# Another start for the first unit's triangular inverse, extra matmuls ahead of idle stretches, and new planner constants

## The chip, the core and the metric

The kernel runs on one core of one Trainium2 chip. The metric is the device time of one execution in microseconds. Over three runs the median was 804.33 us (802.57 to 809.08). One further execution was profiled: it took 806.73 us, and 804.9 us lie between its first and its last instruction (its span). All rows below come from that execution, so sums are made against its 804.9 us.

## What is computed

One transformer-like block over 32 sequences of 256 tokens and 128 features, in four steps, each with a layer norm ahead of it and a residual around it:

```
x = x + attn_a(layernorm(x))      # delta-rule recurrence, below
x = x + ffn(layernorm(x))         # silu(x Wg) * (x Wu), times Wd; hidden 384
x = x + attn_b(layernorm(x))      # Mamba-2 style: conv of 4, silu, chunked state space, gated norm
x = x + ffn(layernorm(x))
```

The change sits in the first step. Its recurrence over the tokens of a sequence is

```
S   = S @ (a_t * (I - b_t * k_t k_t^T)) + b_t * v_t k_t^T
o_t = (q_t @ S) * g_t
```

with a, b and g sigmoids of linear maps of x, and k of unit length. The kernel doesn't walk over tokens. It takes 128 tokens at a time as one chunk, where the recurrence becomes a triangular system: with N the strictly triangular 128x128 matrix of -k_i.k_j times a decay, the inverse X of (I - N) is what the rest of the step multiplies by. Two sequences, so four chunks, are one unit of work, and there are 16 units.

## The kernel before

**Planner.** Every operation of all 16 units goes into a list with its engine, an estimated cost and its predecessors (`Planner.add`, L203; the helpers `matmul`, `transpose`, `act`, `vec`, `pool`, `dma` call it, so the lines that the profile shows are theirs: L238 matmul, L251 transpose, L259 and L261 ScalarE, L275 VectorE, L292 GpSimd, L302 DMA issue). `Planner.run` (L333) then places the operations one by one on PE, DVE, ACT, POOL and the SP queue: of those that could start first, the one with the smallest due time. The due time comes from a unit's place (`at`, L328: period times unit, plus SHIFT of that unit), the longest path to the unit's end, and STAGE for the four steps. HOP is the time that it assumes for a dependence between engines, SLACK the time until a buffer is free again, SWITCH the penalty for a ScalarE table load, KEEP the penalty for a change between matmuls of wide and of narrow weights, EARLY how long before its operands are ready an operation may claim a PSUM bank. Each engine executes its instructions in the planned order, so a wait holds back all that is queued behind it. At the end the order is sorted by planned start and emitted (L441).

**Inverse of a unit** (`attention`, L737). The matrices N of the four chunks stand side by side as `neg_a`. The 16x16 diagonal blocks are inverted by substitution: 8 DMAs on SP write the blocks to DRAM (`blocks_a`, L854), 8 more bring them back, one copy for each of 16 partitions (`rows_a`, L861); then VectorE does 15 pairs of small operations, one pair for each row of a block (`step_a`, `u_a`, L871); GpSimd spreads the result with the mask `blk` into the 128x128 inverse (`x_a`, L881). Then a loop over LEVELS = (16, 32) doubles the block size (L891):

```
for lv, d in enumerate(LEVELS):
    ...                                   # 4 transposes of x_a -> pt_a (PE)
    copy(t_halves[..., 1, :], pt...)      # ACT
    ...                                   # 4 matmuls neg_a, t_a -> p_a (PE)
    copy(t_halves[..., 0, :], p1)         # ACT
    ...                                   # 4 matmuls t_a, x_a -> p_a (PE)
    vec("copy_predicated", halves[..., 1, :], mask_x[lv], p3, ...)   # DVE, into x_a
```

A last level of 64 is written out separately (with `pair`), and then `wq_a`, `z_a`, `po_a`, `py_a` lead to the step's output x1, whose feed-forward step begins with the matmuls `fg_f`.

With SHIFT[0] = 18900 and SHIFT[1] = -4200 against a period of 17900, unit 1 is due before unit 0, and goes first through all of this. The plan is built twice, once for a second path (matmuls with unrounded weights) that these inputs don't take.

Of the kernel before, what the change touches and what calls it, by code (L numbers as in the profile page):

```python
# [11 lines left out]
I32 = mybir.dt.int32  # L12
# [10 lines left out]
BLOCK = 16  # L23
NBLK = P // BLOCK
LEVELS = (16, 32)
HALF = P // 2


# [119 lines left out]
class Planner:  # L148
# [2 lines left out]


    SLOTS = {"ps": 8, "m": 56, "l": 10, "t": 12, "s": 64, "d": 6, "g": 6, "b": 3, "e": 4}
    SWITCH = 76800.0
    HOP, SLACK = 30.0, 130.0
    STAGE = (0.0, -8900.0, 1900.0, 0.0)
    EARLY = 0.0
    SPARE = {"ps": 0.5, "m": 3, "l": 0.5, "t": 1, "s": 2, "d": 0.5, "g": 0.5, "b": 0.5, "e": 0.5}
    LAST = 0.12
    SHIFT = (18900.0, -4200.0, 0.0, 0.0, 1500.0, 11400.0, 1600.0, 1500.0, 0.0, 0.0, 19300.0, -27800.0, -1400.0, -9200.0, -7200.0, -5400.0)  # L160
    HALF = "be"
    RATE = 270.0
    LANES = 8
    CUT = 150.0
    KEEP = 3900.0
    SIZES = {"ps": 512, "m": 512, "l": 1024, "t": 64, "s": 32, "d": 512, "g": 8192, "b": 384, "e": 12288}

    def __init__(self, tc, pools, period, window):
# [34 lines left out]
    def add(self, eng, busy, late, emit, outs, ins, table=None, after=(), lock=False):  # L203
        op = Op()
        op.eng, op.busy, op.late, op.emit, op.table, op.lock = eng, busy, late, emit, table, lock
        op.unit, op.n, op.stage = self.unit, len(self.ops), self.stage
        op.preds, op.succs, op.bufs = {p.n: p for p in after}, [], []
        op.moves, op.cut, op.batch = 0.0, 0, ()
# [61 lines left out]
    def copy(self, out, in_):  # L270
        self.act(out, in_, AF.Copy)
# [12 lines left out]
    def pool(self, name, out, *args, ins=(), cost=None, **kw):  # L284
        n = _count(out)
        if cost is None:
            cost = {
                "tensor_tensor": 1.66 * n + 149, "tensor_scalar": n + 260, "tensor_copy": n + 190, "memset": 0.97 * n + 60,
            }.get(name, n / 2 + 100)

        def emit():
            getattr(self.tc.nc.gpsimd, name)(real(out), *map(real, args), **{k: real(v) for k, v in kw.items()})  # L292
# [19 lines left out]
    def gates(self):  # L312
# [7 lines left out]
        for b, ops in users.items():  # L320
# [4 lines left out]
                    of.add(self.ops[n])  # L325
            b.gate = {p for op in ops for p in op.preds.values()} - of

    def at(self, unit):  # L328

        late = max(0, unit - (self.units - 3))  # L330
        return (unit - late + late * self.LAST) * self.period + self.SHIFT[unit]

    def run(self):  # L333
# [105 lines left out]
                oldest += 1  # L439
        self.span = max(op.done for op in ops)  # L440
        order.sort(key=lambda op: (op.start, op.n))  # L441
        with self.tc.manual_schedule():
            for op in order:
                for b in op.bufs:
                    if b.tile is None:
                        size = self.SIZES[b.kind]
                        flat = self.pools[b.kind].tile([1 if b.kind in "dge" else P, size], BF16 if b.kind in self.HALF else F32, tag=f"{b.kind}{b.slot[1]}", name=b.name + self.mark)
                        b.tile = flat[:, : b.size]
# [13 lines left out]
def hybrid_block(ctx: ExitStack, tc: tile.TileContext, ins: dict, out: bass.AP):  # L462
# [43 lines left out]
            pattern=pattern, channel_multiplier=by,  # L506
        )

    ident = pl.const([P, P], "ident")
    pool("memset", ident, 0.0)  # L510
    select(ident, ALU.not_equal, 0, [[-1, P]], 1, fill=1.0)

# [14 lines left out]

    mask_x = []  # L530
    for d in LEVELS:
        nb = P // (2 * d)
        m = pl.const([P, nb, d], f"m_{d}")
        pool("memset", m, 1.0)
        select(m, ALU.is_ge, 0, [[-2 * d, nb], [0, d]], 1)
        select(m, ALU.is_ge, d - 1, [[2 * d, nb], [0, d]], -1)
        mask_x.append(m.bitcast(I32)[:, None, :, :].to_broadcast([P, NT, nb, d]))

# [156 lines left out]
    def bc(t, n):  # L695

        return t[:, None, :].to_broadcast([P, n, t.shape[1]])
# [39 lines left out]
    def attention(g, x):  # L737
# [113 lines left out]

        blocks = pl.buf("g", [1, NBLK * NT * BLOCK * BLOCK], f"blocks_{n}")  # L854
        for b in range(NBLK):
            at = slice(b * BLOCK, (b + 1) * BLOCK)
            pl.dma(
                blocks[0, :].rearrange("(b t j i) -> b j t i", b=NBLK, t=NT, i=BLOCK)[b, :, :, :],
                diag[:, :, at].part(at), late=1400,
            )  # L860
        rows_n = pl.buf("l", [P, NT, BLOCK, BLOCK], f"rows_{n}")  # L861
        spread = rows_n.rearrange("p t j i -> p (t j i)")
        for b in range(NBLK):
            at = slice(b * BLOCK, (b + 1) * BLOCK)
            size = NT * BLOCK * BLOCK
            pl.dma(
                spread.part(at),
                blocks[0, b * size : (b + 1) * size].via(lambda ap: ap.partition_broadcast(BLOCK)),
                late=2100,
            )  # L870
        u = pl.buf("t", [P, NT, BLOCK], f"u_{n}")  # L871
        pool("tensor_copy", u, bc(eye, NT), cost=254)
        for j in range(BLOCK - 1):
            w = BLOCK - 1 - j
            step = pl.buf("t", [P, NT, w], f"step_{n}_{j}")
            vec(
                "tensor_tensor", step, rows_n[:, :, j, j + 1 :],
                u[:, :, j : j + 1].to_broadcast([P, NT, w]), ALU.mult,
            )
            vec("tensor_tensor", u[:, :, j + 1 :], u[:, :, j + 1 :], step, ALU.add)  # L880
        xi = big([P, 2, SEQS, P], f"x_{n}")  # L881
        xi_f = xi.rearrange("p c s t -> p (c s) t")
        pool(
            "tensor_tensor", xi_f.rearrange("p t (b i) -> p t b i", b=NBLK),
            u[:, :, None, :].to_broadcast([P, NT, NBLK, BLOCK]),
            blk[:, None, :, :].to_broadcast([P, NT, NBLK, BLOCK]), ALU.mult, cost=1215,
        )

        for lv, d in enumerate(LEVELS):  # L891
            nb = P // (2 * d)
            halves = xi_f.rearrange("p t (b h e) -> p t b h e", h=2, e=d)
            pt = bank([P, NT, P], f"pt_{n}_{d}")
            for j in range(NT):
                pl.transpose(pt[:, j, :], xi_f[:, j, :], ident)

            t = big([P, NT, P], f"t_{n}_{d}")
            t_halves = t.rearrange("p t (b h e) -> p t b h e", h=2, e=d)
            copy(t_halves[:, :, :, 1, :], pt.rearrange("p t (b h e) -> p t b h e", h=2, e=d)[:, :, :, 0, :])  # L900
            p1 = bank([P, NT, nb, d], f"p1_{n}_{d}")
# [6 lines left out]
            vec("copy_predicated", halves[:, :, :, 1, :], mask_x[lv], p3, ins=(xi_f,), more=17)  # L908

# [333 lines left out]
```

## Time and profile before

| what | us |
|---|---|
| median of three runs (range) | 804.33 (802.57 to 809.08) |
| profiled execution / its span | 806.73 / 804.9 |
| PE busy | 744.7 |
| DVE busy | 684.3 |
| ACT busy | 597.2 |
| of it 66 table loads of 1283 ns | 84.7 |
| POOL busy | 364.0 |
| 240 + 240 `step_a` and `u_a` on DVE, 216 and 227 ns | 106.0 |
| mean granted TensorE clock | 0.975 |

A busy time is the sum over an engine's instructions. A matmul in float32 appears as two records, and the records of a row overlap, so the time that PE needs for work is better read from the distance of starts than from the durations. The profile's stretches of time list, for each engine, busy us with the number of instructions in brackets, then the clock that TensorE was granted (1.00 is full), the DMA share and GB/s. In the timeline a row gives start, duration, engine, line, operation, out<-in, shapes and count, and in square brackets the idle time before it with what ended it.

Where PE was idle (length of a stretch less PE busy in it): 9.9 us in 0 to 40, 12.1 in 40 to 80, 1.4 in 80 to 120, 4.7 in 120 to 160, some 18 in the 560 us from 160 to 720, and 14.3 from 720 to the end.

### The profile page before, as it was taken

The numbers are of one execution on the slowest core, as the hardware profiler recorded it, in microseconds if no ns is written. First come the engines' busy times: TensorE is split into PE (matmuls) and PEld (weight loads), VectorE is DVE, ScalarE is ACT, GpSimd is POOL, SyncE is SP. The second block draws the span as 40 slices with busy tenths as digits, with TensorE's granted clock in tenths as the row PEclk, the third lists the DMA queues.
The fourth block names the chain that finished last, engine by engine and source line by source line (L and its number), as shares of the span: only waits on it lengthen the run. The fifth ranks groups of instructions, "written<-read, shape, count | busy, mean of one in ns | idle before, by whom it ended". The sixth has DMA issues, their size and how long they took to land.

```text
span 804.9 us, 16786 instructions
## 1 busy us (share of the span) xinstructions
PE 744.7 (93%) x5485; PEld 616.5 (77%) x5485; DVE 684.3 (85%) x2386; ACT 597.2 (74%) x1443; POOL 364.0 (45%) x597
## 2 busy tenths in 40 slices
PE   5958999899999999999999999899999999998886
PEld 4646886687878888877988878686789988776775
DVE  4794799989988889889999689989898778999964
ACT  5833467979687877779787798897955578997862
POOL 8994332262452815514732634646631123243550
PEclk9976999999999999999999999999999999999999
DMA  5221110010110002101011002011201000000001
GB/s 145 82 68 42 29 42 1 5 33 1 56 30 24 22 7 67 42 27 33 18 30 31 27 15 58 16 45 44 67 4 43 14 5 1 5 15 5 13 10 44
DMA packets 42159, 25.48 MB, mean 32 GB/s; under 512 B 18448, under 2 KB 37840, under 8 KB 42064
## 3 DMA queue, kind: packets, MB, share of 16 engines
q1 hardware_dynamic: 41056, 24.13, 11.1%
q8 instruction: 45, 0.74, 0.4%
q14 instruction: 50, 0.41, 0.2%
q10 hardware_dynamic: 1008, 0.20, 0.1%
HBM read 19.16 MB, written 5.14 MB: 30 GB/s over the span
## 4 chain that ended last, share of the span: by engine, by line
PE 52%; DVE 20%; ACT 15%; POOL 5%; issue 3%; DMA 2%; SPq 1%; ACTq 0%; DVEq 0%; POOLq 0%
PE p_a L238 6%; PE fy_f L238 5%; DVE cy_s L275 4%; PE fy_h L238 4%; PE fg_f L238 3%; ACT L261 3%; PE sy_ps_s L238 3%; PE so_s L238 2%; PE fu_f L238 2%; PE pc_s L238 2%; PE fg_h L238 2%; PE fu_h L238 2%; PE pt_a L251 2%; DVE u_a L275 2%; PE cb_ps_s L238 2%
## 5 line engine op out<-in xcount | busy, mean ns | idle before, releaser
L275 DVE SCALAR_TENSOR_TENSOR cy_s<-pc_s,cw,cy_s 128x510 f32<-128x510 f32 (+2 forms) x192 | 137.6, 731 | 2.9 <-ACT cy_s L261 2.3
L261 ACT ACT_TABLE_LOAD x66 | 84.7, 1283 | 9.9 <-DMA x<-in_L_attn_a_x_dram 5.8
L238 PE MATMUL fy_f<-wdT,hT_f 128*128 128x128 f32 x384 | 74.5, 280 | 0.0
L238 PE MATMUL fy_h<-wdT,hT_h 128*128 128x128 f32 x384 | 72.1, 281 | 0.6 <-DVE hT_h L275 0.3
L238 PEld LDWEIGHTS fy_f<-wdT,hT_f 128*128 128x128 f32 x384 | 61.4, 191 | 6.3 <-issue 3.6
L238 PE MATMUL pc_s<-xT_s,w_xbc 128*128 128x512 f32 x128 | 64.5, 599 | 1.3 <-ACT gT_s L259 0.7
L238 PEld LDWEIGHTS fy_h<-wdT,hT_h 128*128 128x128 f32 x384 | 59.1, 191 | 8.1 <-issue 4.3
L275 DVE TENSOR_TENSOR step_a<-rows_a,u_a 128x16 f32<-128x16 f32 (+14 forms) x240 | 51.7, 216 | 7.5 <-DMA rows_a<-blocks_a 3.1
L275 DVE TENSOR_TENSOR u_a<-u_a,step_a 128x16 f32<-128x16 f32 (+14 forms) x240 | 54.3, 227 | 3.9
L261 ACT ACTIVATE cy_s<-pc_s,cb,cw 128x512 f32<-128x512 f32 x64 | 48.3, 779 | 9.3 <-PE pc_s L238 9.1
L292 POOL TENSOR_TENSOR xd_s<-xt_s,dt_s 128x512 f32<-128x512 f32 x32 | 33.2, 1045 | 42.9 <-ACT xt_s L259 42.2
L238 PE MATMUL so_s<-w_out,gT_s 128*128 128x128 f32 x256 | 45.8, 290 | 1.9 <-DVE cy_s L275 1.2
L238 PEld LDWEIGHTS so_s<-w_out,gT_s 128*128 128x128 f32 x256 | 39.7, 204 | 6.6 <-ACT cy_s L261 1.4
L261 ACT ACTIVATE sc_s<-cy_s 128x512 f32<-128x512 f32 x64 | 38.9, 636 | 3.6 <-DVE cy_s L275 1.9
L275 DVE SCALAR_TENSOR_TENSOR sm_s<-pl_s,cb_s 128x512 f32<-128x512 f32 x64 | 41.3, 680 | 0.3 <-ACT pl_s L261 0.2
L292 POOL TENSOR_TENSOR sy_s<-sy_s,yo_s 128x256 f32<-128x256 f32 x32 | 24.6, 773 | 35.5 <-DVE sy_s L275 14.2
L238 PEld LDWEIGHTS p_a<-t_a,neg_a 128*128 128x128 f32 x256 | 36.4, 203 | 5.5 <-ACT t_a L259 3.7
L238 PE MATMUL p_a<-t_a,neg_a 128*128 128x64 f32 x256 | 38.1, 280 | 1.8 <-DVE x L275 1.3
L238 PEld LDWEIGHTS p_a<-x_a,t_a 128*128 128x128 f32 x256 | 36.6, 201 | 3.7 <-ACT t_a L259 2.3
L238 PE MATMUL p_a<-x_a,t_a 128*128 128x64 f32 x256 | 37.9, 274 | 1.0 <-ACT t_a L259 1.0
L259 ACT COPY t_a<-pt_a 128x256 f32<-128x256 f32 (+1 forms) x64 | 20.2, 316 | 24.0 <-PE pt_a L251 22.9
L275 DVE TENSOR_TENSOR hT_f<-fth_f,fu_f 128x512 f32<-128x512 f32 x48 | 31.2, 681 | 7.3 <-PE fu_f L238 4.8
(253 smaller groups left out, 2420.7 us busy)
## 6 DMA issues: line engine op xcount, KB each, us to landing
rows_a<-blocks_a SPq DMA_DIRECT2D x128, 64.0 KB
x<-in_L_attn_a_x_dram SPq DMA_DIRECT2D x16, 256.0 KB
dec_a<-row_a SPq DMA_DIRECT2D x16, 256.0 KB
out_dram<-x SPq DMA_DIRECT2D x16, 256.0 KB
blocks_a<-neg_a SPq DMA_DIRECT2D x128, 4.0 KB
cuts_s<-cut_s SPq DMA_DIRECT2D x48, 8.0 KB
sums_t<-cuts_s SPq DMA_DIRECT2D x32, 12.0 KB
sums_s<-cuts_s SPq DMA_DIRECT2D x16, 24.0 KB
```

Source lines behind the costliest of these rows:

```text
L238: self.tc.nc.tensor.matmul(real(out), lhsT=real(lhsT), rhs=real(rhs), start=start, stop=stop)
L251: self.tc.nc.tensor.transpose(real(out), real(in_), real(ident))
L259: self.tc.nc.scalar.copy(real(out), real(in_))
L261: self.tc.nc.scalar.activation(real(out), real(in_), func, bias=real(bias), scale=real(scale), **kw)
L275: getattr(self.tc.nc.vector, name)(real(out), *map(real, args), **{k: real(v) for k, v in kw.items()})
L292: getattr(self.tc.nc.gpsimd, name)(real(out), *map(real, args), **{k: real(v) for k, v in kw.items()})
```

## The change

1. The unit with g = 0 no longer uses substitution. Its inverse starts as the identity (a ScalarE copy), the elements beside the diagonal of the 2x2 blocks are put in by one `copy_predicated`, and the loop over levels runs over 2, 4, 8, 16, 32 in place of 16, 32. So for this unit 16 DMAs on SP, 30 VectorE operations and two GpSimd operations go, and 3 levels (each with 12 PE operations, 2 ScalarE copies and 1 VectorE copy), a ScalarE copy and a VectorE copy come. GpSimd makes four more masks (4 memsets, 8 selects).
2. `keep_busy` walks over PE's planned order. Where the plan has PE idle for over 300 ns ahead of an operation that is the first to write its PSUM bank, it puts int(0.7 gap / 223) matmuls of the identity with itself into that bank just before it. They come to 122 in the path that runs: 20 ahead of PE's first operation, 10 more up to unit 0's first `fg_f`, 92 later (7 of these with 8 columns, the others with 128).
3. Planner constants: SWITCH, HOP, SLACK, STAGE, EARLY, LAST, SHIFT, KEEP. Unit 0 now goes first. The order of instructions changes on every engine; ACT's table loads go from 66 to 74.

```
+EARLY_UNITS = 1
+EARLY_LEVELS = (1, 2, 4, 8)
...
-    SWITCH = 76800.0
-    HOP, SLACK = 30.0, 130.0
-    STAGE = (0.0, -8900.0, 1900.0, 0.0)
-    EARLY = 0.0
+    SWITCH = 118100.0
+    HOP, SLACK = 70.0, 70.0
+    STAGE = (-1800.0, -7600.0, 1900.0, 0.0)
+    EARLY = 700.0
...
-    LAST = 0.12
-    SHIFT = (18900.0, -4200.0, 0.0, 0.0, 1500.0, 11400.0, 1600.0, 1500.0, 0.0, 0.0, 19300.0, -27800.0, -1400.0, -9200.0, -7200.0, -5400.0)
+    LAST = 0.1
+    SHIFT = (17000.0, 3100.0, 0.0, 0.0, 1500.0, 11400.0, 1600.0, 1500.0, -4200.0, 0.0, 6700.0, -27800.0, -1400.0, -9200.0, -7200.0, -6000.0)
...
-    KEEP = 3900.0
+    IDLE, WARM = 300.0, 0.7
+    KEEP = 2000.0
...
+    def keep_busy(self, order):
+        written, free = set(), 1700.0
+        for op in order:
+            if op.eng != "PE":
+                continue
+            bank = next(b for b in op.bufs if b.kind == "ps")
+            gap = op.start - free
+            if gap > self.IDLE and bank not in written and not op.cut:
+                op.warm, op.bank = int(gap * self.WARM / 223), bank
+            written.add(bank)
+            free = op.start + op.busy
...
+                for _ in range(op.warm):
+                    n = min(P, op.bank.size)
+                    one = self.ident.real()
+                    self.tc.nc.tensor.matmul(op.bank.flat[:, :n], lhsT=one, rhs=one[:, :n], start=True, stop=True)
                 op.emit()
...
-    for d in LEVELS:
+    for d in EARLY_LEVELS + LEVELS:
...
+        if g < EARLY_UNITS:
+            copy(xi_f, bc(ident, NT))
+            later = lambda v: v.rearrange("p t (b h e) -> p t b h e", h=2, e=1)[:, :, :, 1, :]
+            vec("copy_predicated", later(xi_f), mask_x[1], later(diag), ins=(xi_f,), more=17)
+        else:
...
-        for lv, d in enumerate(LEVELS):
+        for d in (EARLY_LEVELS[1:] if g < EARLY_UNITS else ()) + LEVELS:
```

The branch after `else` is the substitution as it was.

More of the change, by code (lines that the diff above doesn't have):

```diff
@@ L207, in add @@
         op.preds, op.succs, op.bufs = {p.n: p for p in after}, [], []
-        op.moves, op.cut, op.batch = 0.0, 0, ()
+        op.moves, op.cut, op.batch, op.warm = 0.0, 0, (), 0
         for v, write in [(v, False) for v in ins] + [(v, True) for v in outs]:
@@ L441, in run @@
         order.sort(key=lambda op: (op.start, op.n))
+        self.keep_busy(order)
         with self.tc.manual_schedule():
@@ L447, in run @@
                         flat = self.pools[b.kind].tile([1 if b.kind in "dge" else P, size], BF16 if b.kind in self.HALF else F32, tag=f"{b.kind}{b.slot[1]}", name=b.name + self.mark)
-                        b.tile = flat[:, : b.size]
+                        b.flat = b.tile = flat[:, : b.size]
                         if len(b.dims) > 2:
@@ L507, in select @@
         )
-    ident = pl.const([P, P], "ident")
+    ident = pl.ident = pl.const([P, P], "ident")
     pool("memset", ident, 0.0)
@@ L526, in hybrid_block @@
     vec("tensor_reduce", eye, ident.rearrange("p (b i) -> p i b", i=BLOCK), AX.X, ALU.add, n=P)
-    mask_x = []
-    for d in LEVELS:
+    mask_x = {}
+    for d in EARLY_LEVELS + LEVELS:
         nb = P // (2 * d)
@@ L536, in hybrid_block @@
         select(m, ALU.is_ge, d - 1, [[2 * d, nb], [0, d]], -1)
-        mask_x.append(m.bitcast(I32)[:, None, :, :].to_broadcast([P, NT, nb, d]))
+        mask_x[d] = m.bitcast(I32)[:, None, :, :].to_broadcast([P, NT, nb, d])
     parts = 2 * NH * 3
@@ L849, in attention @@
         diag = neg[:, :2, :, :].rearrange("p c s t -> p (c s) t")
[L854 to L880, printed above, removed]
@@ L881, in attention @@
         xi = big([P, 2, SEQS, P], f"x_{n}")
         xi_f = xi.rearrange("p c s t -> p (c s) t")
[L883 to L887, printed above, removed]
-        for lv, d in enumerate(LEVELS):
+        if g < EARLY_UNITS:
[3 more added lines that the diff above has]
+        else:
+            blocks = pl.buf("g", [1, NBLK * NT * BLOCK * BLOCK], f"blocks_{n}")
+            for b in range(NBLK):
+                at = slice(b * BLOCK, (b + 1) * BLOCK)
+                pl.dma(
+                    blocks[0, :].rearrange("(b t j i) -> b j t i", b=NBLK, t=NT, i=BLOCK)[b, :, :, :],
+                    diag[:, :, at].part(at), late=1400,
+                )
+            rows_n = pl.buf("l", [P, NT, BLOCK, BLOCK], f"rows_{n}")
+            spread = rows_n.rearrange("p t j i -> p (t j i)")
+            for b in range(NBLK):
+                at = slice(b * BLOCK, (b + 1) * BLOCK)
+                size = NT * BLOCK * BLOCK
+                pl.dma(
+                    spread.part(at),
+                    blocks[0, b * size : (b + 1) * size].via(lambda ap: ap.partition_broadcast(BLOCK)),
+                    late=2100,
+                )
+            u = pl.buf("t", [P, NT, BLOCK], f"u_{n}")
+            pool("tensor_copy", u, bc(eye, NT), cost=254)
+            for j in range(BLOCK - 1):
+                w = BLOCK - 1 - j
+                step = pl.buf("t", [P, NT, w], f"step_{n}_{j}")
+                vec(
+                    "tensor_tensor", step, rows_n[:, :, j, j + 1 :],
+                    u[:, :, j : j + 1].to_broadcast([P, NT, w]), ALU.mult,
+                )
+                vec("tensor_tensor", u[:, :, j + 1 :], u[:, :, j + 1 :], step, ALU.add)
+            pool(
+                "tensor_tensor", xi_f.rearrange("p t (b i) -> p t b i", b=NBLK),
+                u[:, :, None, :].to_broadcast([P, NT, NBLK, BLOCK]),
+                blk[:, None, :, :].to_broadcast([P, NT, NBLK, BLOCK]), ALU.mult, cost=1215,
+            )
@@ L907, in attention @@
                 matmul(p3[:, j, :, :], t[:, j, :], halves[:, j, :, 1, :], True, True)
-            vec("copy_predicated", halves[:, :, :, 1, :], mask_x[lv], p3, ins=(xi_f,), more=17)
+            vec("copy_predicated", halves[:, :, :, 1, :], mask_x[d], p3, ins=(xi_f,), more=17)
         up, low = slice(0, HALF), slice(HALF, P)
```

## The prediction

> **What bounds the kernel now.** I read the page first: PE is busy 93% of the span, DVE 85%. Then its slices, because a mean over stages hides where the rest lies.
>
> ```profile
> PE   5958999899999999999999999899999999998886
> DVE  4794799989988889889999689989898778999964
> PEclk9976999999999999999999999999999999999999
> ```
>
> From the fifth slice (80 us) to the last four PE is full: there PE bounds the kernel, and only less PE work, fewer small stalls or a faster clock help. The weak slices are the first four, and the clock is low in the third and fourth. So next the stretches around each drop of the clock:
>
> ```profile
> 44.50:47.90 3.40, 0.59 (x4) 0.42 (x4) 3.19 (x7) 0.00 (x0) 3.25 (x5) 1.00 0.50 146
> 47.90:58.10 10.20, 6.25 (x22) 4.92 (x22) 9.90 (x28) 2.82 (x6) 10.08 (x16) 0.50 0.21 68
> 61.60:65.00 3.40, 1.53 (x7) 0.65 (x6) 3.23 (x15) 1.83 (x11) 1.21 (x6) 0.99 0.04 4
> 65.00:78.60 13.60, 12.30 (x54) 11.27 (x55) 4.12 (x16) 3.65 (x11) 8.53 (x11) 0.50 0.22 61
> ```
>
> The first number behind the length is PE's busy time, the last but two the clock. PE was 17% and 45% busy in the 3.4 us ahead of two drops, then ran 10.2 and 13.6 us at half speed. What PE waited for is in the timeline of the four engines and SP:
>
> ```profile
> 31.42 3.62 SPq L302 DMA_DIRECT2D blocks_a<-neg_a  x8
> 35.08 3.67 SPq L302 DMA_DIRECT2D rows_a<-blocks_a  x8
> ...
> 41.30 0.64 DVE L275 TENSOR_TENSOR step_a<-rows_a,u_a 128x60 f32<-128x60 f32 x1 [0.22 <-DMA blocks_a<-neg_a]
> ...
> 54.93 0.50 DVE L275 TENSOR_TENSOR u_a<-u_a,step_a 128x4 f32<-128x4 f32 x1
> ...
> 57.18 1.25 POOL L292 TENSOR_TENSOR x_a<-u_a,blk 128x512 f32<-128x512 f32 x1
> ...
> 61.11 0.60 PE L251 MATMUL pt_a<-ident,x_a 128*128 128x128 f32 x4
> ...
> 103.61 0.72 PE L238 MATMUL fg_f<-xT_f,wgT 128*128 128x512 f32 x2
> ```
>
> The first unit's `neg_a` (unit 1 is first in the old order, unit 0 in the new) is ready at 31.4 us. Its 16 DMAs, 30 DVE operations and the GpSimd spread take until 58.4, and level 16 starts at 61.1. The first feed-forward matmul starts at 103.6.
>
> **What PE's work costs.** Distances of starts, at full clock: a float32 matmul of 128 columns takes two records and 0.21 us (four `fy_h` at 790.36, 0.84 to the next start), a 64-column one of the levels no less (four in 0.94 at 99.42); I use 0.22 for both, and 0.11 for a transpose (four in 0.44 at 109.75). At half clock the 128-column matmul takes 0.43 (row at 14.57, four matmuls in 1.74 to the next start), so PE is cold until about 17 us, although the clock column has no record there.
>
> ```profile
> 14.57 1.95 PE L238 MATMUL pk_a<-wkab,xT_a 128*128 128x131 f32 x8
> 16.31 1.46 PE L251 MATMUL xT_ps_a<-ident,xn_a 128*128 128x128 f32 x8
> ...
> 99.42 1.10 PE L238 MATMUL p_a<-t_a,neg_a 128*128 128x64 f32 x8
> 100.36 0.44 PE L238 MATMUL kk_a<-kT_a 128*128 128x128 f32 x2
> ```
>
> Counting the instructions of the two orders at such distances (0.86 for 512 float32 columns, 0.43 for 256, 0.23 for an `fg`/`fu` matmul), the program before holds 680 us of PE work, 62 of it ahead of the first `fg_f`. That starts at 103.6, so 41 us are lost by then; the other 618 take 701 us.
>
> **Part 1, the first unit.** Gone: 3.62 + 3.67 us of SP issue with their landing, 30 DVE operations of 216 to 227 ns (6.6 us), two GpSimd operations. Added: 3 levels. A level at full clock is the row of `pt_a` at 82.18 up to the end of `copy_predicated` at 86.81, 4.6 us; at half clock, 61.11 to 69.90, 8.8. I take 4.6, since PE has other units' work between the steps and fillers: `neg_a` at about 32 (its chain is unchanged, but some more bn statistics are queued ahead on DVE), the first element step 1 us, 3 x 4.6 = 14, so level 16 starts at 47 to 48, not 61.1. From there to `fg_f` the trace took 42.5 us, 13.6 of them at half clock with 12.3 busy. At full clock 6.2 of that goes; also 1.5 to 2 of the idle rows between. That gives 47.5 + 34 = 82 for `fg_f`. A check from the work: 64 us stand ahead of it in the new order, with 10 fillers (2 us) after PE's first operation; from 8 us on that makes 74 without any stall, so 82 leaves 8 us for stalls. Gain 21.6; the ends are 9.0 (three levels at 8.8: `fg_f` at 94.6) and 25.6 (half the stalls: 78). SP: the second unit's `blocks_a` no longer queue behind the first unit's 16 DMAs (issued at 38.86, their `neg_a` ready at 35.6), and its DVE pairs come in 36 to 57 us, so its level 16 can follow when the first unit's level 64 ends. SP's wait for the scalar `large` moves: it stood behind both units' blocks, and now stands ahead of `dec_a` of unit 2 and of unit 1's blocks. DVE writes `large` at 40.93 now, from a matmul at 40.61 that the new order has ahead of the first `kk_a`, so before 31; I cost it at nothing, and if it were late, unit 1 would be, while unit 0's levels fill PE. The identity copy (ACT, about 0.6) runs while ACT waits for x, idle until 5.80; the 12 more mask operations (0.15 to 0.26 each, some 2.5 us) move POOL's first `rstd_a`, which waited for DVE statistics at 6.25 and now gets about 1 us late: that is inside the stall allowance. Behind the first `fg_f`, PE has 623 us of work where it had 618: +5.0.
>
> **Part 2, fillers.** 20 ahead of PE's first real matmul (8.05 now) start at about 1.7 us, when `ident` is there; at half clock 0.43 x 20 = 8.7 ends at 10.4, at full clock 6.1. With a clock that rises on the way they end about when the weights land: cost 0 to 2.4 us, taken 0 (ends by 8.5); PE's cold stretch to 17 us goes, about 3 us of PE time, which is within the 82. The 92 later ones: 85 x 0.22 plus 7 small ones, 19 to 20 us. In a real gap they cost nothing; on a busy PE all. PE's own idle after 103.6 is some 37 us, so most have room, but the plan's gaps need not be there. I take a quarter, +5 (ends 0 and 20). They write only to the bank of the operation behind them, so they add no wait, just length.
>
> Against that stands the clock. Later drops:
>
> ```profile
> 727.20:730.60 3.40, 1.39 (x13) 1.08 (x11) 3.40 (x11) 3.40 (x10) 3.21 (x5) 0.99 0.00 0
> 730.60:734.00 3.40, 3.24 (x10) 2.36 (x11) 3.19 (x12) 2.42 (x8) 1.85 (x3) 0.50 0.00 0
> ```
>
> and the same at 242.4, 754.5 and 771.5, PE busy 3.1 to 3.4 in each: 13.2 us of busy PE at half clock, 6.6 lost. I take -5 of them (0 to -6.6). Here a rule speaks against the fills. The Trainium skill, "TensorE: Matmul & The Clock Gate", section "Why this matters for your kernels", has the clock fall when PE idles for over some 3 us between bursts. By it the gap of 4.48 us ahead of 47.31 costs clock, but the fills behind the front buy none, the -5 goes and the sum gives 794. The trace differs: ahead of 65.0 the longest idle row is 0.92 us, ahead of 242.4 it is 1.07, and yet the clock fell, after 3.4 us with PE 45% and 63% busy. So I follow the rows: share of work, not one long gap.
>
> **Part 3, new order.** 8 more table loads of 1283 ns are 10.3 us of ACT, which has 26% idle and carries 15% of the chain that ended last: +1.5 (0 to 10). The rest of the order (HOP, SLACK, due times) I can't cost from the trace: the stages follow each other after the same amount of PE work in both orders to within 10 us, so 0, with -8 to +8 for it: of the 701 us after `fg_f`, 83 are not work by my distances, and a tenth of that either way is my guess.
>
> **Sum.** -21.6 + 5.0 + 5 - 5 + 1.5 = -15.1 against 804.9 of span. The profiled run is 2.4 us above the median, so from 804.33: 789.
>
> **Rivals.** (a) The front's gain is given back: 16 units pass DVE, 80 to 90% busy and more from 80 us on, and what starts 20 us earlier waits there. For it: DVE at 95% in 360 to 440. Against: it loses 6.6 us of work, and PE, not DVE, is full in those slices, idle for 1 to 4 us in each 80. If two thirds of the 21.6 are lost: 804.3 - 15.1 + 14.4 = 804. (b) Slower: the fillers and the doubling fall on a busy PE. 92 fillers at full price 20, doubling 5.0, table loads on the chain 10.3: 35 against 21.6 from the front and 5 of clock: 804.3 - 26.6 + 35.3 = 813. It decides from where more than two thirds of the planned gaps are not real while ACT's loads hold PE up. For it: the plan's 223 ns for a matmul is what PE takes, but it allows for no micro-stalls, so PE may be late at most places. Against: other engines are late then too. (c) The change doesn't do what it says: fillers late, the clock falls as before, levels at 8.8: `fg_f` at 94.6, so gain 9.0, the clock's 5 gone as well: 804.3 - 9.0 + 5.0 + 5 + 1.5 = 807.
>
> **How the numbers follow.** Forecast with its spread (775 to 796) 0.75; (a) 0.09, (c) 0.07, (b) 0.09. 1% of 804.33 is 8, about what a measurement tells from no change: below 796.3 is faster, above 812.4 slower. Faster: the forecast's 0.75 and a little of (a): 0.76. Slower: most of (b) and a little of (c), with the order's +8: 0.09. Same: 0.15. The range reaches from the good ends (front 4 more, fillers 5 less, order -8: 772) to (a) and near (c): 773 to 806.
>
> **What would show it.** The first `fg_f` near 82 (over 92: part 1 failed). No `blocks_a` ahead of unit 1's; level 16 of unit 0 near 48. Granted clock 1.00 from about 10 us to 720. PE idle below 12 us in 0 to 80, most of it ahead of 8 us. After `fg_f` some 707 us to the end; far more means fillers on a busy PE or a worse order, which a longer ACT chain in the windows would tell apart. I am wrong if the front comes early and the end does not.

## The result and the profile after

The changed kernel takes 829.18 us (median of 6 runs, 827.82 to 831.02) against 805.61 us for the kernel before on the same chip: ratio 1.0302, 95% interval 1.0274 to 1.0329. The forecast was 789. Times here and below are medians of fast executions; only new_order_only also had slow ones (4 of 20, at a lower granted clock), which are left out. The profiled execution has a span of 829.3 us. The page, busy shares and granted clock in 40 slices, each now 20.7 us:

```profile
span 829.3 us, 17347 instructions
...
PE   6998999989999999999899999999999999987996
...
DVE  3967779999997988698989798699899757889974
...
PEclk8999999999999999999999999999999999999999
```

The weak front is gone as forecast: PE is at 80% or more from the second slice to the 36th, and the clock is below 0.9 in the first slice alone (0.91 in 60 to 80 us; mean over the program 0.987, before 0.975). The kernel is slower all the same. The front in the timelines of PE and DVE, in order of time, with start and length first in each row:

```profile
13.30 1.63 PE L254 MATMUL xT_ps_a<-ident,xn_a 128*128 128x128 f32 x4 [4.72 <-ACT xn_a L264]
...
34.98 1.09 DVE L278 SCALAR_TENSOR_TENSOR neg_a<-kk_a,e_a 128x256 f32<-128x256 f32 x3 [0.24 <-PE kk_a L241]
...
37.39 0.66 PE L254 MATMUL pt_a<-ident,x_a 128*128 128x128 f32 x4 [0.59 <-DVE x_a L278]
...
43.18 0.66 PE L254 MATMUL pt_a<-ident,x_a 128*128 128x128 f32 x4 [0.67 <-DVE x_a L278]
...
49.75 0.60 PE L254 MATMUL pt_a<-ident,x_a 128*128 128x128 f32 x4
...
54.76 0.60 PE L254 MATMUL pt_a<-ident,x_a 128*128 128x128 f32 x4
...
95.08 1.02 PE L241 MATMUL fg_f<-xT_f,wgT 128*128 128x512 f32 x3
```

`neg_a` is complete at 36.07 (34.98 + 1.09) where the prediction had 32, the three levels take 5.8, 6.6 and 5.0 us for 4.6, level 16 of unit 0 starts at 54.76 for 47 to 48, and the first `fg_f` at 95.08 for 82. That is still 8.5 us ahead of the 103.61 of before. From there to the end it is 734.2 us; before it was 701.3.

To see where those go, the document keeps a ledger by the prediction's own method: the PE instructions of the planned order counted at its distances of starts (work), and what the time exceeds them by (loss). Each row is one profiled execution (the runs below the second row are explained with the experiments); losses are read at a unit's first feed-forward matmul and at the end of the span. Fillers count as work.

```
                     span   work | loss by: first  unit 3  unit 8  unit 15   end
                                            fg_f    fg_f    fg_f    fg_f
before               804.9  680.0            41.4    54.2    75.0    94.9   124.9
after                829.3  713.9            24.6    37.2    58.1    85.9   115.4
no_fillers           831.7  686.7            33.7    54.2    74.5   106.6   145.0
kept_order_unit_1    804.5  686.7            35.3    48.2    67.6    89.4   117.8
fitted_no_fillers    795.9  686.7            29.5    39.5    59.2    77.2   109.2
fitted_with_fillers  787.9  702.0            21.3    28.5    46.8    62.6    85.9
late_identity        784.9  702.0            17.0    24.2    42.7    58.5    82.9
```

The change's 122 fillers are 27.2 us of the 713.9. Without them (no_fillers, the first experiment) the ledger is plain: 6.7 us of doubling as work, 7.7 us less loss at the first `fg_f`, all of it given back by unit 3 (54.2 in both), and 20.6 us of new loss between unit 8 and the end (145.0 - 74.5 = 70.5 against 124.9 - 75.0 = 49.9). The windows of two stretches there show PE. Columns: length, busy time of PE, weight loads, DVE, ACT and POOL, granted clock, DMA share, GB/s. Before:

```profile
400.00:500.00 100.00, 98.11 (x745) 83.31 (x744) 86.69 (x302) 81.58 (x195) 40.60 (x65) 1.00 0.12 32
700.00:780.00 80.00, 71.20 (x595) 55.49 (x593) 73.14 (x225) 68.00 (x151) 39.33 (x57) 0.94 0.04 11
```

After:

```profile
400.00:500.00 100.00, 94.30 (x701) 76.61 (x700) 89.31 (x332) 84.12 (x185) 40.61 (x65) 1.00 0.10 27
700.00:780.00 80.00, 71.28 (x512) 54.05 (x509) 69.01 (x210) 66.63 (x129) 24.13 (x34) 0.98 0.03 8
```

In 400 to 500 PE is busy 3.8 us less than before, at full clock, and the busy time of after has fillers in it. No other engine is full in its place: DVE is at 89%, ACT at 84%. PE's losses are many and small. One of the larger, in the timeline of PE:

```profile
758.58 1.38 PE L475 MATMUL fg_h<-ident 128*128 128x128 f32 x10 [1.63 <-DVE xr_h L278]
759.71 0.47 PE L241 MATMUL fg_h<-xT_h,wgT 128*128 128x512 f32 x1
```

The ten records are five fillers. They did not fill the idle 1.63 us, they stand behind it: their bank is free only when `xr_h` is done, which the `fg_h` behind them waits for too. In no_fillers the same `fg_h` waits the same 1.63 us and then starts at once:

```profile
762.49 0.79 PE L241 MATMUL fg_h<-xT_h,wgT 128*128 128x512 f32 x1 [1.63 <-DVE xr_h L278]
```

So a filler can wait where the prediction said it adds no wait, and here five of them add about 1.1 us.

### The profile page after: what moved, and what is told of

It is laid out like the page before. It is cut to its first block, busy times and chain, and to the rows that moved or that the text cites. A ratio compares the mean times of both kernels' runs of the same rounds, so it can differ in the third digit from the quotient of the medians.

```text
span 829.3 us, 17347 instructions
## 1 busy us (share of the span) xinstructions
PE 774.0 (93%) x5789; PEld 644.1 (78%) x5789; DVE 682.9 (82%) x2360; ACT 610.7 (74%) x1458; POOL 361.4 (44%) x607
## 4 chain that ended last, share of the span: by engine, by line
PE 42%; DVE 28%; ACT 17%; issue 4%; SPq 3%; DMA 3%; POOL 2%; ACTq 0%; DVEq 0%; POOLq 0%
DVE cy_s L278 6%; PE p_a L241 5%; ACT L264 4%; SPq L305 3%; PE pc_s L241 3%; PE fy_f L241 2%; PE fy_h L241 2%; DVE sm_s L278 2%; DVE step_a L278 2%; DVE x L278 2%; PE sy_ps_s L241 2%; DVE u_a L278 2%; PE so_s L241 2%; PE fu_h L241 2%; PE fg_h L241 2%
## 5 line engine op out<-in xcount | busy, mean ns | idle before, releaser
L241 PE MATMUL fy_h<-wdT,hT_h 128*128 128x128 f32 x384 | 70.3, 280 | 0.4 <-DVE hT_h L278 0.2
L264 ACT ACTIVATE cy_s<-pc_s,cb,cw 128x512 f32<-128x512 f32 x64 | 48.8, 782 | 17.9 <-PE pc_s L241 17.4
L278 DVE TENSOR_TENSOR step_a<-rows_a,u_a 128x40 f32<-128x40 f32 (+14 forms) x225 | 51.4, 230 | 6.6 <-DMA rows_a<-blocks_a 3.0
L278 DVE TENSOR_TENSOR u_a<-u_a,step_a 128x40 f32<-128x40 f32 (+14 forms) x225 | 48.3, 216 | 2.6
L241 PE MATMUL so_s<-w_out,gT_s 128*128 128x128 f32 x256 | 41.7, 278 | 0.1
L254 PE MATMUL pt_a<-ident,x_a 128*128 128x128 f32 x204 | 33.9, 277 | 5.9 <-DVE x_a L278 3.0
L241 PE MATMUL sy_ps_s<-xd_s,sm_s 128*64 128x64 f32 x1024 | 35.8, 228 | 3.0 <-DVE sm_s L278 1.8
L241 PEld LDWEIGHTS sy_ps_s<-xd_s,sm_s 128*64 128x64 f32 x1024 | 32.8, 142 | 7.4 <-DVE sm_s L278 3.5
```

Source lines behind the costliest of these rows:

```text
L241: self.tc.nc.tensor.matmul(real(out), lhsT=real(lhsT), rhs=real(rhs), start=start, stop=stop)
L254: self.tc.nc.tensor.transpose(real(out), real(in_), real(ident))
L264: self.tc.nc.scalar.activation(real(out), real(in_), func, bias=real(bias), scale=real(scale), **kw)
L278: getattr(self.tc.nc.vector, name)(real(out), *map(real, args), **{k: real(v) for k, v in kw.items()})
```

## The experiments

Two theories to begin with. A: the kernel's planner orders the whole program anew for any change in its list of operations or its constants; the constants of before were fitted to its own list, and a plan that isn't fitted costs more than the change brings. B: what the change adds does it: doubling and fillers on a busy PE, table loads, the front colliding with DVE.

### One part at a time

The change has three parts: the new constants, the doubling, the fillers. `no_fillers` and `new_order_only`:

```diff
-        self.keep_busy(order)
# new_order_only, also
-EARLY_UNITS = 1
+EARLY_UNITS = 0
-    for d in EARLY_LEVELS + LEVELS:
+    for d in LEVELS:
```

`fillers_only` and `doubling_only` have the constants of before (SWITCH 76800, HOP, SLACK 30, 130 and the rest) with one of the other parts.

> The changed kernel without the fillers; the plan and with it every other instruction's place stay the same. 122 fillers at 0.22 us are 27 us of PE work. Theory 1, fillers on a busy PE are the cost: about 829 - 22 = 807 (20 of the 27 us come after PE's first operation and nearly all count), or a bit less. Theory 2, the new order is the cost and the fillers stand in waits that are there anyway: 826 to 832, and the clock drops more often than 0.987 as a mean. Theory 3, the fillers keep the clock up and so pay: over 832.

> Only the planner's constants of the change; substitution for all units, no fillers. Theory 1: near the kernel before, 800 to 808. Theory 2: 820 to 832. If the front of the first unit is what the change won, this is slower than the changed kernel without fillers by 5 us or more.

> The kernel before with keep_busy added to its own plan, 113 fillers or so of 0.22 us, 50 of them before 60 us, where PE idles. Theory 1: the ones after 100 us, some 60, add up to 13 us, less what the clock gives at the front (up to 9 us): 800 to 815. Theory 2: no more than the kernel before, 795 to 805, for the fillers are in real gaps.

> The kernel before with only the new start of unit 0's inverse, which in the old order is the second unit. 6.7 us of PE work more, 16 DMAs and 30 VectorE operations fewer. If PE's work is what counts: 804 + 5 = 809; if the front gains what the prediction said: 790 to 800. A replanned order alone can move it by some us either way.

```
                 median us  ratio to before [95% interval]
no_fillers         833.8    1.0350 [1.0282, 1.0418]
new_order_only     812.7    1.0076 [1.0046, 1.0105]
fillers_only       808.9    1.0044 [1.0018, 1.0069]
doubling_only      823.4    1.0204 [1.0136, 1.0272]
```

The fillers are not what makes the change slow: by the medians it is 4.6 us faster with them (829.2 for 833.8, though the two intervals overlap), while before loses 0.4% by them. new_order_only lies between the two ranges that were expected of it, and doubling_only is above both of its own. The granted clock of no_fillers, in 40 slices, has the drops that the fillers take away (ninth slice, and the 36th and 37th):

```profile
PEclk9999999989999999999999999999999999988999
```

The doubling alone costs 2.0%, 18 us, of which its work explains 6.7. Whether the other 11 or 12 come from the doubling or from the plan that it is ordered by, these four can't tell.

### A new plan with no new work

Three nudges of the kernel before, each of one constant by one, and the doubling on unit 1, the first unit in the order before. Nothing is added to or taken from the work in the nudges.

```diff
-    HOP, SLACK = 30.0, 130.0
+    HOP, SLACK = 31.0, 130.0     # hop_31
+    HOP, SLACK = 30.0, 131.0     # slack_131
-    RATE = 270.0
+    RATE = 269.0                 # rate_269
-        if g < EARLY_UNITS:
+        if g == 1:                # doubling_unit_1
```

> The kernel before, with nothing but the planner's HOP at 31 in place of 30 ns. No work is added or taken away; about a fifth of PE's rows stand elsewhere. Theory A, any replanning loses what the tuned constants had won (a plan is good only for the list of operations that it was tuned on): 812 to 825, as with the doubling alone (823). Theory B, the doubling itself is what costs: 801 to 808, as before.

> The kernel before, with nothing but SLACK at 131 in place of 130 ns; a third of PE's rows stand elsewhere. Theory A: 812 to 825. Theory B: 801 to 808.

> The kernel before, with nothing but the DMA rate that the planner assumes at 269 in place of 270. Theory A: 812 to 825. Theory B: 801 to 808.

> The kernel before with the doubling on unit 1, the one that goes first in the old order, in place of unit 0; no fillers. If the front is what counts, its first feed-forward comes some 10 us earlier and the end with it: 790 to 798. Theory A: the front comes early and the end is 812 to 825 all the same. Theory B, the doubling as such costs: 815 to 825 with a slow stage at the front.

```
                 median us  ratio to before [95% interval]
hop_31             811.6    1.0073 [1.0049, 1.0097]
slack_131          819.7    1.0179 [1.0141, 1.0218]
rate_269           810.2    1.0065 [1.0040, 1.0090]
doubling_unit_1    827.4    1.0266 [1.0229, 1.0304]
```

All three nudges are slower, by 0.7 to 1.8%. Two of them stay just under the 812 to 825 that A named, and all are above B's 801 to 808. One nanosecond in SLACK costs nearly as much as doubling_only. The loss of slack_131 at its end is 137.7 us with the work of before, that of doubling_only 138.2: by this sum the doubling's plan is no worse than a plan that one nanosecond has upset.

### The doubling with the order kept

The test that tells A from B: plan with the substitution, then take the substitution of one unit out of the finished order and put its doubling in, at its due places. On PE, 36 instructions are added and no other changes its place. (Two comments stand for the code of `put_in`.) The 12 operations for the new masks go into POOL's order too, from 20 us of plan on.

```diff
         order.sort(key=lambda op: (op.start, op.n))
+        order = self.put_in(order)
...
+    def put_in(self, order):
+        # starts of the doubling follow each other from the end of neg_a, x 1.2
+        order = [op for op in order if not op.gone] + self.chain
+        order.sort(key=lambda op: (op.start, op.n))
+        # its buffers take slots that are free over their places in the order
```

With them went a nudge of the changed kernel, and before with the 21 fillers behind 660 us of its plan alone.

> The kernel before with its order of work kept: the plan is made with the substitution, then the substitution of unit 0 is taken out and the doubling of unit 0 is put in at its due places; every other instruction keeps its place (on PE the order is that of before plus 36 instructions). doubling_only has the same work with a new plan: 823.4. Theory A (most of doubling's cost is the new plan): 6.7 us more PE work, the other losses as before, 124.9, up to 8 us less of them in the front: 804 to 812. Rival (doubling itself costs it: its work, and an earlier front that runs into DVE): 820 or more.

> The same with unit 1, the first unit in the order before. doubling_unit_1 has the same work with a new plan: 827.4. Theory A: 804 to 812, with the first fg_f near 98 in place of 103.6. Rival: 820 or more. If the first fg_f comes at 98 and the end is at 811 or above, the front's gain is given back behind it even with the order kept.

> The changed kernel with HOP 71 in place of 70: no work added or removed, another plan. Theory A (the changed kernel's plan is an ordinary one, not a tuned one): within 5 of 829, either way. Rival (its constants were fitted to its own list, as those of before were to theirs): 835 to 843, as the nudges of before cost 5 to 14.

> The kernel before with fillers only behind 660 us of its plan (21 of the 114). In fillers_only the stretch from the first fg_h of unit 12 to that of unit 13 took 38.3 us in place of 41.5, while the fillers ahead of it cost 9. If the fillers pay where the clock fell (727, 754 and 771 us), 801 to 804. If they only lengthen the tail: 807 to 810.

```
                   median us  ratio to before [95% interval]
kept_order_unit_0    811.7    1.0089 [1.0054, 1.0125]
kept_order_unit_1    806.8    1.0022 [1.0001, 1.0043]
hop_71               830.6    1.0333 [1.0279, 1.0386]
tail_fillers         807.2    1.0036 [1.0014, 1.0058]
```

The same doubling costs 0.2% with the order kept and 2.7% with a new plan (unit 1), 0.9% and 2.0% (unit 0). So A holds: by the ratios 2.4% and 1.2%, some 20 and 9 us, are the new plan's. hop_71 suggests that the changed kernel has an ordinary plan already: this nudge leaves it where it was. tail_fillers brought nothing.

A's time holds, but its front doesn't: with the order kept nothing comes earlier. The timeline of PE in kept_order_unit_1:

```profile
53.30 0.66 PE L265 MATMUL pt_a<-ident,x_a 128*128 128x128 f32 x4 [0.41 <-DVE x_a L289]
...
59.04 1.62 PE L265 MATMUL xT_ps_a<-ident,xn_a 128*128 128x128 f32 x4 [1.72 <-ACT xn_a L275]
61.34 0.80 PE L252 MATMUL pk_a<-wkab,xT_a 128*128 128x131 f32 x2 [0.68 <-ACT xT_a L273]
...
69.38 0.60 PE L265 MATMUL pt_a<-ident,x_a 128*128 128x128 f32 x4
...
104.19 0.71 PE L252 MATMUL fg_f<-xT_f,wgT 128*128 128x512 f32 x2
```

Level 8 starts at 53.30 (the first row) and its matmuls are issued by 57.3, but level 16 (the `pt_a` at 69.38) stands where the order of before has it, behind the transposes and matmuls of later units. The first `fg_f` comes at 104.19, before it was 103.61. The gaps of the front take up the 6.7 us of work, and no more. Part of that is this build's own. Before, POOL had the first unit's `k_a` at 25.30:

```profile
25.30 1.04 POOL L292 TENSOR_TENSOR k_a<-k_a,rk_a 128x512 f32<-128x512 f32 x1
```

In kept_order_unit_1 the 12 mask operations (4.6 us on POOL between 22.23 and 29.44) stand ahead of it, and PE waits:

```profile
27.06 0.97 POOL L306 TENSOR_SCALAR_AFFINE_SELECT m<-m 128x64 f32<-128x64 f32 x2
...
29.40 1.03 POOL L306 TENSOR_TENSOR k_a<-k_a,rk_a 128x512 f32<-128x512 f32 x1
...
30.49 1.12 PE L265 MATMUL kT_ps_a<-ident,k_a 128*128 128x128 f32 x4 [4.12 <-POOL k_a L306]
```

The first unit's `neg_a` is then complete at 37.00, before it was 31.39; in kept_order_unit_0 PE waits the same 4.12 us. So the two kept orders are, if anything, slower than the doubling needs, which leaves A standing; what a kept order gains with the masks elsewhere was not run. The gains that were measured all came with a new order and fitted constants.

### A plan fitted to the doubling

The planner works out an end for each plan from its own costs. It is not a time of the chip, but it orders the runs fairly well: 754.0 for before, 762.5 for hop_31, 767.7 for slack_131 and doubling_only, 771.1 for the change (755.8 for new_order_only and 751.0 for fitted_before, below, are too kind). Moving SWITCH, STAGE, LAST, KEEP and the due times of SHIFT by random steps, and keeping what brought that end forward, gave 737.5 for the list with the doubling:

```diff
-    SWITCH = 118100.0
+    SWITCH = 234100.0
-    STAGE = (-1800.0, -7600.0, 1900.0, 0.0)
+    STAGE = (-1800.0, -7600.0, 2300.0, 0.0)
-    LAST = 0.1
+    LAST = 0.132
-    SHIFT = (17000.0, 3100.0, 0.0, 0.0, 1500.0, 11400.0, 1600.0, ..., -27800.0, -1400.0, -9200.0, -7200.0, -6000.0)
+    SHIFT = (17000.0, 700.0, 0.0, -3700.0, 1500.0, 11400.0, -300.0, ..., -27400.0, -400.0, -9200.0, -6600.0, -7500.0)
-    KEEP = 2000.0
+    KEEP = 1900.0
```

`fitted_with_fillers` is the change with these constants and nothing else; its plan has fewer or shorter gaps, so `keep_busy` puts in 69 fillers, not 122. `fitted_no_doubling` and `fitted_before` are the controls: the list without the doubling, fitted from the constants of the change and from those of before. `second_fit` is another search for the list with the doubling. (fitted_no_doubling and second_fit also have another HOP, 20 and 50.)

> The doubling of unit 0 without fillers, as in no_fillers (833.8), with the due times, SWITCH, LAST and KEEP fitted to this list of operations; HOP, SLACK and EARLY as in the change. The kernel's planner works out an end for each plan: 754.0 us for before, 771.1 for the change, 737.5 for this one. If the change lost because its plan is an ordinary one: as no_fillers less 17 to 34 (half to all of the 33.6 between the two plans), 800 to 817. If the doubling loses by itself: 825 to 834 in any plan.

> The same plan with the change's fillers: the change with other constants only. Fillers gave 4.6 us to the change and cost before 3.5. If they pay in whatever plan has the doubling: 3 to 6 below fitted_no_fillers. If they pay only where a plan has real gaps, and the fitted one has few: 0 to 4 above it.

> No doubling and no fillers, as new_order_only (814.1), with constants fitted to that list (HOP 20 among them, so its planned end of 744.8 is on cheaper hops and no better than 751 at the same ones). If fitting a plan is worth more than the change itself: 797 to 808, at or below before. If a better planned end does not carry to the chip: 810 to 820.

> The kernel before (no doubling, no fillers, HOP and SLACK as they were) with SWITCH, KEEP and a few due times fitted on, in about as many trials as the doubling had: planned end 751.0 for 754.0. If the list without the doubling has little left to gain: 799 to 806. If any list gains some 10 us from more fitting, and the doubling has no part in fitted_no_fillers: 790 to 797.

> The doubling without fillers again, with constants of a second, independent search (planned end 742.9, HOP 50). If the doubling with a fitted plan is what gains: 793 to 803. If fitted_no_fillers was one lucky plan: 806 to 825.

```
                     median us  ratio to before [95% interval]
fitted_no_fillers      794.8    0.9853 [0.9815, 0.9892]
fitted_with_fillers    791.7    0.9837 [0.9803, 0.9870]
fitted_no_doubling     801.4    0.9960 [0.9942, 0.9977]
fitted_before          807.4    1.0024 [0.9999, 1.0049]
second_fit             796.0    0.9860 [0.9818, 0.9901]
```

The clean pair is without fillers: exactly the operations of no_fillers, ordered by other constants, take 794.8 us in place of 833.8, below the 800 to 817 that A expected. (Only ACT's table loads, which follow from the order, differ: 67 for 73 at the activations' line.) With fillers it is 791.7 in place of 829.2. So the order is what made the change slow. What in an order costs the time, beyond many small waits of PE, these runs don't show.

Two separate fits of the list with the doubling agree (0.985 and 0.986), and the lists without it come to 0.996 and 1.002: a difference of about 1%. (By the searches' own count they tried some 3,100 and 1,400 plans with the doubling, 1,400 and 2,600 for the two controls; a longer search of those could bring them nearer.) That the doubling earns this 1% by an earlier front is not shown, for the control's front is as early:

```profile
96.25 0.95 PE L241 MATMUL fg_f<-xT_f,wgT 128*128 128x512 f32 x3
96.64 0.96 PE L241 MATMUL fg_f<-xT_f,wgT 128*128 128x512 f32 x3
```

The first row is fitted_no_fillers, with some 67 us of PE's work ahead of it by the ledger's distances, 6.7 of them the doubling; the second is fitted_no_doubling, with some 61. The 4.1 us between their profiled spans (795.9 and 800.0) arise behind these rows, where the two lists hold nearly the same work, and may be a matter of the two plans. The fits with the doubling still have the early identity copy, of which the last experiment tells.

In the ledger the fitted plan's lead at the first `fg_f` holds to the end (fitted_no_fillers: 11.9 us less loss than before at the first `fg_f`, 17.7 at unit 15, 15.7 at the end). The same windows as above in fitted_with_fillers:

```profile
400.00:500.00 100.00, 98.47 (x769) 84.89 (x770) 83.38 (x306) 80.40 (x190) 41.27 (x68) 1.00 0.12 32
700.00:780.00 80.00, 74.09 (x612) 60.85 (x613) 66.36 (x191) 63.10 (x134) 32.26 (x47) 0.98 0.04 11
```

PE is busy 98.47 of 100 us and 74.09 of 80, where the change has 94.30 and 71.28. The fillers' 3 us lie within the two intervals.

### The identity copy

One step of the front was still open: `neg_a` at 36.07 in place of 31.4. ACT's timeline, before:

```profile
2.69 0.45 ACTq L302 DMA_DIRECT2D bab<-in_L_attn_a_bb_dram  x1
4.25 0.33 ACTq L302 DMA_DIRECT2D bk<-in_L_attn_a_bk_dram  x1
5.43 0.34 ACTq L302 DMA_DIRECT2D wg<-in_L_attn_a_Wg_dram  x1
5.80 1.28 ACT L261 ACT_TABLE_LOAD   x1 [5.80 <-DMA x<-in_L_attn_a_x_dram]
8.26 1.65 ACT L261 ACTIVATE xn_a<-x,shift_a,rstd_a 128x128 f32<-128x128 f32 x4 [1.18 <-DVE shift_a L275]
```

and after:

```profile
2.69 1.28 ACT L262 ACT_TABLE_LOAD   x1 [2.69 <-issue]
3.98 0.62 ACT L262 COPY x_a<-ident 128x512 f32<-128x512 f32 x1
9.12 0.33 ACTq L305 DMA_DIRECT2D bab<-in_L_attn_a_bb_dram  x1
9.93 0.34 ACTq L305 DMA_DIRECT2D bk<-in_L_attn_a_bk_dram  x1
12.31 0.34 ACTq L305 DMA_DIRECT2D wg<-in_L_attn_a_Wg_dram  x1
12.75 2.03 ACT L264 ACTIVATE xn_a<-x,shift_a,rstd_a 128x128 f32<-128x128 f32 x5 [8.15 <-DMA x<-in_L_attn_a_x_dram]
```

ACTq rows are DMAs that ACT issues. The identity copy, with its table load, came ahead of the last three weight loads; these then went out at 9.12, 9.93 and 12.31 instead of 2.69, 4.25 and 5.43, and the first `xn_a`, queued behind them, started at 12.75 instead of 8.26. The last run moves that copy alone, in fitted_with_fillers:

```diff
             copy(xi_f, bc(ident, NT))
+            pl.ops[-1].defer = True
...
+        for op in ops:
+            if getattr(op, "defer", False):
+                op.start = min(s.start for s in op.succs) - 1500.0
         order.sort(key=lambda op: (op.start, op.n))
```

> fitted_with_fillers (791.7) with one thing moved: unit 0's identity copy on ACT stands 1.5 us of plan ahead of its first use, and no longer ahead of the last three of ACT's seven weight loads and of the first xn_a. In the change those three loads were issued at 9.1, 9.9 and 12.3 us (2.7, 4.3 and 5.4 before) and xn_a started at 12.75 (8.26 before). If the copy's place caused that: xn_a near 8.3, neg_a and the first fg_f 2 to 4.5 us earlier (93.5 to 89-91.5), total 786 to 791. If something else held the loads up: xn_a still at 12.5 or later and 790 to 793.

It takes 786.8 us, ratio 0.9794 [0.9768, 0.9820]: the fastest of all. (Its interval and that of fitted_with_fillers, 0.9803 to 0.9870, just overlap; none of its five runs is as slow as the fastest of the other's six.) ACT's timeline in it, then the copy, PE's first level, and the first `fg_f`:

```profile
2.69 0.45 ACTq L305 DMA_DIRECT2D bab<-in_L_attn_a_bb_dram  x1
...
5.17 0.34 ACTq L305 DMA_DIRECT2D wg<-in_L_attn_a_Wg_dram  x1
...
8.87 2.12 ACT L264 ACTIVATE xn_a<-x,shift_a,rstd_a 128x128 f32<-128x128 f32 x5 [2.06 <-DVE shift_a L278]
...
27.22 0.61 ACT L262 COPY x_a<-ident 128x512 f32<-128x512 f32 x1
...
30.00 0.63 PE L254 MATMUL pt_a<-ident,x_a 128*128 128x128 f32 x4 [0.67 <-DVE x_a L278]
...
89.18 0.94 PE L241 MATMUL fg_f<-xT_f,wgT 128*128 128x512 f32 x3
```

The loads are back at 2.69 to 5.17, the level at 30.00 stood at 34.28 in fitted_with_fillers, and the first `fg_f` at 93.46: 4.3 us earlier, and still 4.1 at unit 15. `neg_a` is complete at 28.77, where it was 33.06. The copy's place, with the table load that it brings, was the cause. Why the loads then waited until 9 us, 4.5 us behind the copy's end, the trace doesn't show.

## Why the prediction was wrong

**Part 3, the order: the step that failed.** "The rest of the order (HOP, SLACK, due times) I can't cost from the trace ... so 0, with -8 to +8 for it." It was the largest term of all. Behind the first `fg_f` no_fillers has 622.8 us of work (before 617.8) and 111.3 of loss (before 83.5): +27.8 for a term put at nothing, over three times its stated end. (In the change itself fillers stand in part of those waits: 90.8 of loss and some 20 of fillers, in the same 734 us.) With other constants the same operations lose 79.7 there (fitted_no_fillers), so the excess is the order's. The argument behind the zero, stages that follow each other after the same amount of PE work, compares positions in two lists and says nothing of how long PE waits between them. The planner itself had a figure that the prediction didn't use: its planned end is 771.1 us for the change and 754.0 for before, 17 us the wrong way. And the order was taken for a separate part: it comes with the doubling even where all constants stay, some 9 and 20 us in doubling_only and doubling_unit_1 against the kept orders. The table loads, costed at 1.5 us in the same part, were not measured by themselves, but their number doesn't order the runs: hop_31 and slack_131 have 62 and are slower than before with 66, second_fit has 75 beside that of the identity copy and is among the fastest.

**Part 1, the first unit.** The mechanism is right, the size was not. From `neg_a` to level 16 the first unit takes 18.7 us (36.07 to 54.76) where it took 29.7, but the gain at the first `fg_f` is 8.5 us (6.0 without fillers) for 21.6. Of the 13.1 that are missing, 4.1 stand ahead of `neg_a`: "the identity copy ... runs while ACT waits for x" looked at ACT's busy time and not at the DMA issues queued behind the copy (moving it was worth 4.3 us in the fitted plan; in the change itself it was not moved). Some 3.2 are in the levels, which PE, shared with other units, takes in 17.4 us for three instead of 14. The last 5.8 lie between level 16 and `fg_f`, 40.3 us instead of 34.5. POOL's masks were sized rightly: its first `rstd_a` starts at 7.13, 0.9 later. The 5.0 us of work behind `fg_f` are right.

**Part 2, fillers and clock.** Net 0 was forecast, +5 and -5. By the medians they gave 4.6 to the change, and took 0.4% from before. The clock rose as said (0.976 without them, 0.987 with them). The rule of the Trainium skill against PE pauses over some 3 us ("TensorE: Matmul & The Clock Gate", "Why this matters for your kernels"), taken as the only cause, would have left it: in the three slices of no_fillers where the clock was low PE's longest pause is 1.67 us, and with fillers those slices show 0.9 or more. The gain is in the front: fillers bring the first `fg_f` from 97.61 to 95.08 and unit 3's from 191.90 to 185.05, and by the end 2.4 us of 6.9 are left in the profiled pair. "They add no wait" failed at places like 758.58.

**The rivals.** (a), the front's gain given back, did happen, but not by its mechanism: DVE is less busy in 100 to 200 us than before, and with fitted constants the gain stays. (b) foretold the right side for the wrong reason. That a plan which isn't fitted may lose 1 to 2% by itself was not among the rivals, and should have been the first: the constants are quoted to the nanosecond in the kernel, and their list is what the change breaks.

**With the plan put right** the sum was near: fitted_with_fillers, the same operations but for 53 fillers fewer, takes 791.7 against the 789 forecast. That is partly luck, since its first `fg_f` comes 10 us earlier and not 21.6, and the rest comes behind it.

## What to carry to other kernels

Where a greedy planner with fitted constants orders the work, a change of the work is two changes: keep the order and measure the edit alone, then fit the constants again and measure that, with a control that is fitted as long without the edit. Constants fitted to the old list can make a new one look bad. Where the planner works out an end, compare it before and after. Nudge one constant by one before you believe a difference of 2%: here it moved the time by 0.7 to 1.8%. When an operation is put early "while the engine is idle", look at what the engine issues behind it, DMAs first.

## What the runs showed of the hardware

- Three weight loads that ACT issues went out from 4.5 us after the end of a 0.62 us copy that, with its 1.28 us table load, was put ahead of them (4.60 to 9.12), where without it the first went out at 2.69: a small operation between DMA issues can cost far more than its length.
- Twenty fillers at the very start took 6.70 us, between the 8.6 of half clock and the 4.4 of full clock (estimates from the 0.43 and 0.22 us of a matmul before). PE then idled 4.72 us in the change, and four `pk_a` matmuls at 15.60 took 1.90 us to the next start; in late_identity, where PE was busy 17.64 of the first 20 us, the four at 11.58 took 0.99. The clock column has 0.83 and 1.00 for these 20 us; it is no sure witness so early, since it has 1.00 before as well, where PE ran at half speed until about 17 us.
